# Seven products of quarters for the output projection, in one PSUM bank, and three shared staging buffers, in a two-layer transformer kernel

## The chip, the cores and the metric

One core of a Trainium2 chip runs the whole program. The metric is the device time of one execution in microseconds (us). All data are float32. In the text PE is TensorE (matmuls) and PEld its weight loads, DVE is VectorE, ACT is ScalarE, POOL is GpSimd, and SP is the engine whose queue issues nearly all DMAs.

## The reference

The kernel computes two layers for 4 batches of 1,024 rows of 512 features. The first is a graph attention with few neighbours, and the change does not touch it. The second is a transformer block with modulation:

```python
mod = silu(c) @ W_mod + b_mod
sh_msa, sc_msa, g_msa, sh_mlp, sc_mlp, g_mlp = split(mod, 6)
x = x + g_msa * attention(modulate(layernorm(x), sh_msa, sc_msa), W_qkv, W_out, b_out)
x = x + g_mlp * ff(modulate(layernorm(x), sh_mlp, sc_mlp), W1, b1, W2, b2)

# attention: 16 heads of 64
q, k, v = split(x @ W_qkv, 3)
attn = softmax(einsum('bqhd,bkhd->bhqk', q, k) * 64 ** -0.5)
out = einsum('bhqk,bkhd->bqhd', attn, v).reshape(B, T, 1024) @ W_out + b_out
```

What is changed is the last product, `@ W_out`, with the addition to the residual rows, and the staging of the softmax weights on their way to the product with `v`.

## The kernel before, in words

The attention stage goes through 256 slots: 4 batches, 8 pairs of heads `gp` in each, 8 blocks `t` of 128 query rows in each pair. So a batch has 64 slots, and two pairs of heads make one of four head groups `g`, with 16 slots.

In each slot the program issues, in this order: the transposition of the previous slot's first head on DVE (`turn`, L1119); evacuations of products that were put off (`later`); the scores of two heads into four PSUM banks (`scores`, L1084, tile `psc`); their maxima on DVE (`largest`, L1095); the exponentials with row sums on ACT (`weights`, L1101); reciprocals on DVE (L1106) and the scaling of the weights, the first head on ACT (L1108), the second on POOL (L1110); the transposition of the previous slot's second head; and then the work that a planner has put into this slot (`emit`). The next slot's scores need the banks back, so they wait for the exponentials.

`turn` writes into a staging tile `wd` of two blocks of rows. When the second block is in, four DMAs on SP's queue carry a head's tile to `wT` (L1123). Each of the two heads has two `wd` buffers of its own.

The planner's work in a slot is a list `fill` of entries (earliest slot, latest slot, units, place, function). They are:

- `attend`: the product of four slots earlier's weights with `v` (L1046, tile `pav`, 32 passes of 256 columns, in pairs at the same time), two units, evacuated by ACT into `oT` (L1055).
- `project`: 128 rows of the output projection for one head group (L1064, tile `pout`, four passes of 512 columns), one unit. DVE adds it to the residual rows `xr` (L1072); after the last group the rows are written to `x2d` (L1076) and their statistics taken.
- The chain of steps for q, k and v (`seven`, L520): products of a matrix multiplication by seven products of quarters instead of eight. Steps alternate on two banks `q1` and `q2`; their evacuations are put off to `later`, some on ACT, some on DVE (L534, L538). The sums of quarters of the weights are made on POOL (L491 to L494).
- Small ones: loads, gates, transpositions of normalized rows (`norm_T`, L430).

A matmul of float32 appears as two passes in the trace, so a `project` with two matmuls has four. `pav` and `pout` share the tag `mm` with two banks. `order_chain` chooses slots for the chain by dynamic programming on a cost that grows with the square of a slot's units, `order_others` moves the rest one by one. In a slot the entries are sorted by place: `attend` has 1, `project` 2, `norm_T` 3, gates and statistics 4, and a chain step 0.5, or 2.5 when the slot before also has one. The cost and the place are these:

```python
def cost_of(u, n):
    return u * u + 4 * max(n - 2, 0) ** 2
...
def place(k):
    if k in inside:
        return 2.5 if s - 1 in steps else 0.5
    return fill[k][3]
```

After the slots come the last projections among the first products of the MLP, and then the MLP of eight blocks of 512 rows. It uses the same seven products, with 256 columns.

Of the kernel before, what the change touches and what calls it, by code (L numbers as in the profile page):

```python
# [41 lines left out]
def cond_block_kernel(  # L42
# [880 lines left out]
    ps = pctx.enter_context(tc.tile_pool(name="ps2", bufs=1, space=PSUM))  # L923
    with ExitStack() as actx:
        ap_ = actx.enter_context(tc.tile_pool(name="ap", bufs=1, reuse_waits="tile"))
        MM = dict(tag="mm", bufs=2)
        q1, q2 = (ps.tile([P, F], F32, name=n, tag=n) for n in ("q1", "q2"))
        two_banks = {"ma": q2, "mb": q1, "mc": q1, "md": q2}
        NP = 2 * NGRP
# [6 lines left out]
        wout, gate = {}, {}  # L936
        vt, oT, xr, wn, wd, wT = {}, {}, {}, {}, {}, {}

        def bank(name):
            return ps.tile([P, F], F32, name=name, **MM)  # L940

        turns = []

        def bank_q(name):
# [4 lines left out]

        def load_out(b, g):  # L950

            t = op_.tile([P, 2, F], F32, name="wout", tag="wout", bufs=1)
            nc.sync.dma_start(t, w_out[g * GW : (g + 1) * GW, :].rearrange("(c p) f -> p c f", p=P))
            wout[b, g] = t

# [3 lines left out]
            for p in range(2):  # L959
                nc.gpsimd.tensor_tensor(t[:, p, :], t[:, p, :], gate[b][0], ALU.mult)  # L960

        def load_rows(b, n):

            t = op_.tile([P, F], F32, name="xr", tag="xr", bufs=NT)
            nc.sync.dma_start(t, x1d[b * NT + n])
            xr[b, n] = t

        def gate_rows(b, n):

            nc.gpsimd.tensor_tensor(xr[b, n], xr[b, n], gate[b][1], ALU.add)  # L970


        def gates_of(b):
# [62 lines left out]
                rhs=lambda which, n, c: of_weights(("v", b, g), wv[b, g], which, c),  # L1036
            )

        def attend(b, gp, k):

            po = ps.tile([P, QB], F32, name="pav", **MM)
            g, p = divmod(gp, 2)
            w = wT[b, gp, k]
            for m in range(KC):
                for j in range(2):
                    nc.tensor.matmul(  # L1046
                        po[j * D : (j + 1) * D, :],
                        lhsT=vt[b, g][:, m, p * P + j * D : p * P + (j + 1) * D],
                        rhs=w[:, j, :, m, :],
                        start=(m == 0),  # L1050
                        stop=(m == KC - 1),
                    )
            if k == 0:
                oT[b, gp] = op_.tile([P, S], F32, name="oT", tag="oT", bufs=3)
            nc.scalar.copy(  # L1055
                oT[b, gp][:, k * QB : (k + 1) * QB].rearrange("p (t u q) -> p u t q", t=QT, u=4),
                po.rearrange("p (u t q) -> p u t q", t=QT, u=4),
            )

        def project(b, g, n):  # L1060

            po = ps.tile([P, F], F32, name="pout", **MM)
            for p in range(2):
                nc.tensor.matmul(  # L1064
                    po,
                    lhsT=oT[b, 2 * g + p][:, n * P : (n + 1) * P],
                    rhs=wout[b, g][:, p, :],
                    start=(p == 0),
                    stop=(p == 1),
                )  # L1070
            t = xr[b, n]
            nc.vector.tensor_tensor(t, po, t, ALU.add)  # L1072
            if g == NGRP - 1:
                i = b * NT + n
                statistics(t, mv2[:, i, :], op_)
                nc.sync.dma_start(x2d[i], t)  # L1076


        def scores(b, gp, t):
# [32 lines left out]
        def turn(b, gp, t, j):  # L1112

            k, at = divmod(t, QT)
            if at == 0:
                wd[j] = ap_.tile([P, 4 * KC, QT, U], F32, name="wd", tag=f"wd{j}", bufs=2)
                if j == 0:
                    wT[b, gp, k] = ap_.tile([P, 2, 4, KC, QT * U], F32, name="wT", tag="wT", bufs=2)
            nc.vector.transpose(wd[j][:, :, at, :], wn.pop((b, gp, t, j)).rearrange("p (m k) -> p m k", k=U))  # L1119
            if at == QT - 1:  # L1120
                flat = wd[j].rearrange("p m t q -> p (m t q)")
                for u in range(4):
                    nc.sync.dma_start(  # L1123
                        wT[b, gp, k][:, j, u].rearrange("p m q -> p (m q)"), flat[U * u : U * (u + 1), :]
                    )
# [3 lines left out]
            return lambda: qp.tile([P, S], F32, name="ex", tag=tag, bufs=2)  # L1129

        def home_o():
            return op_.tile([P, S], F32, name="ex", tag="oT", bufs=3)

        def home_v():
            return vp.tile([P, NT, GW], F32, name="hs", tag="v", bufs=2)
# [10 lines left out]
        NS = B * NP * NT  # L1146
        LAG = 4

        chain = []

        def add(lo, hi, units, place, f, *args):
            fill.append((lo, hi, units, place, lambda: f(*args)))
# [15 lines left out]
        for b in range(B):  # L1168
# [22 lines left out]
            for gp in range(NP):  # L1191
# [13 lines left out]

                for k in range(NB):
                    lo = at + QT * k + LAG
                    add(lo, lo + (lo < NS - 8), 2, 1, attend, b, gp, k)
                if p == 1:
                    for n in range(NT):  # L1210
                        lo = at + max(QT * (n // 2) + LAG + 2 + (g == 0), 7)
                        hi = at + 19
                        if at == NS - NT:

                            lo = hi = NS + (-2, -1, -1, 0, 1, 1, 3, 3)[n]
                        add(lo, hi, 1, 2, project, b, g, n)
                if gp == 0:
                    lo = max(at - 1, 0)
                    add(lo, lo, 0, 0, gates_of, b)
                    for n in range(NT):  # L1220

                        lo = at + (1 + n if b == 0 else 14 + n // 2)
                        add(lo, lo, 0, 0, load_rows, b, n)
                        add(lo + 1, lo + 1, 0, 4, gate_rows, b, n)
                if p == 0:
                    add(at + 12, at + 12, 0, 0, load_out, b, g)
                    add(at + 13, at + 13, 0, 4, gate_out, b, g)
        add(3, 3, 0, 4, rstd, rs1, mv1, nm1, NT, NTA)

        add(NS - 20, NS - 20, 0, 4, rstd, rs2, mv2, nm2, 0, 3 * NT)  # L1230
# [20 lines left out]
        add(NS - 7, NS - 7, 0, 0, put_w1_rows)  # L1251
        add(NS - 8, NS - 8, 0, 4, mlp_rows)
        for i in range(4):
            at = NS - (10, 9, 6, 4)[i]
            home = (home_ex, home_q("qT"), home_q("kT"), home_o)[i]
            add(at, at, 0, 4, mlp_weights, nc.gpsimd, i, home)

# [14 lines left out]


        where = [f[0] for f in fill]
        inside = set(chain)

        def takes(k):

            return fill[k][2], int(k not in inside and fill[k][3] in (1, 2))

        def load_of(ks):
            used = {}
# [3 lines left out]
            return used  # L1286

        def cost_of(u, n):
            return u * u + 4 * max(n - 2, 0) ** 2

        def order_chain():

            used = load_of(k for k in range(len(fill)) if k not in inside)
            values = {where[k] for k, f in enumerate(fill) if f[3] == 1}
            first_steps = set(range(0, len(chain), 4))
            best = {(0, 0): (0, ())}
            for s in range(-8, NS):
                new = {}
                for (n, was), (cost, at) in best.items():
                    load, banks = used.get(s, (0, 0))  # L1300
                    for m in range(2):
                        extra = 0
                        if m > 0:
                            if n == len(chain) or not fill[chain[n]][0] <= s <= fill[chain[n]][1]:
                                break
                            load += fill[chain[n]][2]
                            if was and n not in first_steps and s not in values:
                                extra = 3
                        if n + m < len(chain) and fill[chain[n + m]][1] <= s:
                            continue  # L1310
                        c = cost + cost_of(load, banks) + extra
                        if (n + m, m) not in new or c < new[n + m, m][0]:
                            new[n + m, m] = c, (at, (s,) * m)
                best = new
            at = min((best[k] for k in best if k[0] == len(chain)), key=lambda v: v[0])[1]
            slots = []
            while at:
                at, part_ = at
                slots.append(part_)
            for k, s in zip(chain, [s for part_ in reversed(slots) for s in part_]):  # L1320
                where[k] = s
# [21 lines left out]
                    used[where[k]] = used.get(where[k], (0, 0))[0] + u, used.get(where[k], (0, 0))[1] + n  # L1343

        for _ in range(4):
            order_chain()
            order_others()
        for k, n, late in behind:
            where[k] = where[n] + late
# [12 lines left out]
        def emit(a, b):  # L1362


            for s in range(a, b):
                steps = {where[k] for k in chain}

                def place(k):
                    if k in inside:
                        return 2.5 if s - 1 in steps else 0.5  # L1370
                    return fill[k][3]

                for k in sorted(fill_of(s), key=lambda k: (place(k), k)):
                    fill[k][4]()
                if s in steps and s - 1 not in steps and sum(fill[k][2] for k in fill_of(s)) >= 3:
                    while later:
                        later.pop(0)()

        row_sum(0, 2)
        emit(-3, 0)  # L1380
        before = None
        for s in range(NS + 1):
# [4 lines left out]
            if s < NS:  # L1387
                b, r = divmod(s, NP * NT)
                gp, t = divmod(r, NT)
                sc = scores(b, gp, t)  # L1390
                mx = [largest(sc[j]) for j in range(2)]
                ws = [weights(sc[j], mx[j]) for j in range(2)]
                now = ((b, gp, t), ws)
                scaled(0, *ws[0])
# [212 lines left out]
```

## Time and profile before

| | before |
|---|---|
| median of three runs (lowest to highest) | 3060.71 us (3057.65 to 3062.03) |
| profiled execution | 3061.31 us, its span 3059.4 us |
| granted TensorE clock | 0.999 |
| matmuls of the output projection, L1064 | 512 passes, 245.5 us busy, mean 609 ns of one |
| its additions on DVE, L1072 | 128, 85.5 us busy, mean 678 ns |
| transpositions, L1119 | 512, 633.4 us busy |
| scores, L1084 | 415.3 to 2248.6 us of the span |

The durations are of one profiled execution, from the start of its span. Matmuls are pipelined: one lasts longer than the distance to the next, so what one costs is read from the distance of two starts. Idle time of an engine before an instruction is put down to what released it. A row of the timeline gives start, length, engine, line, operation, tiles and how many instructions are merged.

### The profile page before, as it was taken

Reading aid. Unit: us, or ns where it says so; the run is one execution under the profiler, and the core shown is the slowest. Engines: PE = TensorE matmul, PEld = TensorE weight load, DVE = VectorE, ACT = ScalarE, POOL = GpSimd, SP = SyncE. Lnnn points to the kernel's source line nnn. Section 1 sums busy time; section 2 is a strip of 40 time slices with the busy share of each in tenths; the row PEclk is TensorE's granted clock in tenths of the full one; section 3 lists DMA queues with packets and bytes.
Section 4 is the critical chain, followed back from the end, with each engine's and each line's share of the span. In section 5 each row is a group of like instructions: output and inputs, shape, how many; then the busy total and the mean of one; then the engine's idle time right before and its main releaser. Section 6 shows DMA issues by size and latency. Waiting matters only on the chain.

```text
span 3059.4 us, 40809 instructions
## 1 busy us (share of the span) xinstructions
PE 3025.6 (99%) x14967; PEld 1918.2 (63%) x14967; DVE 1957.9 (64%) x2743; ACT 1432.7 (47%) x2367; POOL 1213.8 (40%) x742
## 2 busy tenths in 40 slices
PE   9999999999999999999999999999999999999999
PEld 5666655455455455455455455455468888888888
DVE  3788867777878777878777878777764232222222
ACT  2444456556755555755555756556641221122211
POOL 1444455454555555555545555555531100111010
PEclk9999999999999999999999999999999999999999
DMA  6433448667777777877776877776772010101110
GB/s 194 133 122 112 133 107 199 152 159 179 187 181 189 178 167 170 193 182 183 180 174 159 200 185 174 182 175 152 192 192 93 14 49 28 49 14 42 35 42 14
DMA packets 282714, 418.00 MB, mean 137 GB/s; under 512 B 28912, under 2 KB 101036, under 8 KB 282516
## 3 DMA queue, kind: packets, MB, share of 16 engines
q1 hardware_dynamic: 282268, 415.06, 53.3%
q8 instruction: 120, 1.97, 0.3%
q14 instruction: 78, 0.64, 0.1%
q10 hardware_dynamic: 248, 0.34, 0.0%
HBM read 121.09 MB, written 25.76 MB: 48 GB/s over the span
## 4 chain that ended last, share of the span: by engine, by line
PE 84%; DVE 5%; ACT 3%; issue 2%; POOL 2%; SPq 2%; DMA 2%; POOLq 0%; ACTq 0%; DVEq 0%
PE q L520 18%; PE psc L1084 15%; PE pav L1046 14%; PE pout L1064 7%; PE mbd L520 5%; PE mbu L520 5%; PE mad L520 4%; PE mau L520 3%; PE mcd L520 2%; PE mdd L520 2%; PE mdu L520 2%; PE mcu L520 2%; PE pa L706 1%; ACT w L1101 1%; PE pf L666 1%
## 5 line engine op out<-in xcount | busy, mean ns | idle before, releaser
L1110 POOL TENSOR_SCALAR w<-w,sm 128x1024 f32<-128x1024 f32 x256 | 728.5, 2846 | 845.8 <-DVE sm L1106 844.5
L1101 ACT ACTIVATE w<-psc,mx 128x1024 f32<-128x1024 f32 x512 | 570.6, 1114 | 633.5 <-DVE mx L1095 633.5
L1119 DVE STREAM_TRANSPOSE wd<-w 128x1024 f32<-128x1024 f32 x512 | 633.4, 1237 | 131.5 <-ACT w L1108 117.8
L1095 DVE TENSOR_REDUCE mx<-psc 128x1 f32<-128x1024 f32 x512 | 599.3, 1211 | 123.0 <-PE psc L1084 121.2
L1084 PE MATMUL psc<-kT,qT 64*128 64x512 f32 x2048 | 529.9, 615 | 2.8 <-ACT kT L1010 1.4
L1046 PE MATMUL pav<-wT,v 128*64 128x256 f32 x4096 | 476.2, 382 | 2.0 <-DMA wT<-wd 1.2
L1046 PEld LDWEIGHTS pav<-wT,v 128*64 128x64 f32 x4096 | 294.7, 137 | 221.5 <-issue 66.9
L1084 PEld LDWEIGHTS psc<-kT,qT 64*128 64x128 f32 x2048 | 202.9, 186 | 254.4 <-issue 144.8
L1108 ACT ACTIVATE w<-w,sm 128x1024 f32<-128x1024 f32 x256 | 291.0, 1137 | 0.0
L499 POOL TENSOR_TENSOR tx<-hT 128x512 f32<-128x512 f32 x8 | 10.3, 1286 | 596.7 <-ACT hT L435 596.7
L1064 PE MATMUL pout<-wout,oT 128*128 128x512 f32 x512 | 245.5, 609 | 0.0
L520 PE MATMUL q<-hT,wqk 128*128 128x512 f32 (+1 forms) x396 | 182.6, 585 | 4.4 <-DVE q L534 4.4
L1064 PEld LDWEIGHTS pout<-wout,oT 128*128 128x128 f32 x512 | 90.2, 189 | 134.0 <-issue 119.1
L542 ACT COPY mbu<-mau 128x512 f32<-128x512 f32 x30 | 17.1, 570 | 276.5 <-PE mau L520 276.5
L706 PE MATMUL pa<-kp,sfT 128*128 128x320 f32 x512 | 143.5, 433 | 1.5 <-ACT sfT L681 1.5
L520 PEld LDWEIGHTS q<-hT,wqk 128*128 128x128 f32 x396 | 73.5, 190 | 100.6 <-issue 85.0
L1072 DVE TENSOR_TENSOR xr<-pout,xr 128x512 f32<-128x512 f32 x128 | 85.5, 678 | 79.1 <-PE pout L1064 79.0
L520 PE MATMUL q<-tx,ex 128*128 128x512 f32 (+1 forms) x264 | 125.0, 597 | 1.4 <-POOL tx L499 1.4
L706 PEld LDWEIGHTS pa<-kp,sfT 128*128 128x128 f32 x512 | 94.8, 190 | 38.2 <-ACT sfT L681 1.9
L666 PE MATMUL pf<-wx,xT 128*128 128x512 f32 x256 | 117.1, 601 | 0.0
L520 PE MATMUL mad<-w,hs 128*128 128x256 f32 x512 | 113.1, 379 | 0.0
L520 PEld LDWEIGHTS mad<-w,hs 128*128 128x128 f32 x512 | 97.3, 190 | 13.2
(284 smaller groups left out, 4222.7 us busy)
## 6 DMA issues: line engine op xcount, KB each, us to landing
wT<-wd SPq DMA_DIRECT2D x1024, 256.0 KB
wqk<-in_w_qkv SPq DMA_DIRECT2D x64, 256.0 KB
xT<-in_xt SPq DMA_DIRECT2D x32, 256.0 KB
xs<-in_x SPq DMA_DIRECT2D x32, 256.0 KB
x1d<-xs SPq DMA_DIRECT2D x32, 256.0 KB
xl<-x1d SPq DMA_DIRECT2D x32, 256.0 KB
wv<-in_w_qkv SPq DMA_DIRECT2D x32, 256.0 KB
xr<-x1d SPq DMA_DIRECT2D x32, 256.0 KB
```

Of the source, the lines that this page charges most:

```text
L520: nc.tensor.matmul(t[:, q * width : (q + 1) * width], lhsT=lhs(which, q, k), rhs=rhs(which, q, k), start=(fresh and q == 0 and k == 0), st ...
L666: nc.tensor.matmul(pfs[i], lhsT=xT[i][:, c, :], rhs=wx[:, c, :], start=False, stop=(c == FC - 1), skip_group_check=True,)
L706: nc.tensor.matmul(pas[i][:, n, :HF], lhsT=sfT2[i][:, c, :], rhs=kp[:, b, c, n * HF : (n + 1) * HF], start=False, stop=(c == FC - 1), skip ...
L1046: nc.tensor.matmul(po[j * D : (j + 1) * D, :], lhsT=vt[b, g][:, m, p * P + j * D : p * P + (j + 1) * D], rhs=w[:, j, :, m, :], start=(m == 0),
L1064: nc.tensor.matmul(po, lhsT=oT[b, 2 * g + p][:, n * P : (n + 1) * P], rhs=wout[b, g][:, p, :], start=(p == 0), stop=(p == 1),)
L1072: nc.vector.tensor_tensor(t, po, t, ALU.add)
L1084: nc.tensor.matmul(sc[j][:, n * F : (n + 1) * F], lhsT=qT[b, gp][q, t * P : (t + 1) * P], rhs=kT[b, gp][q, n * F : (n + 1) * F], start=Tru ...
L1095: nc.vector.tensor_reduce(mx, sc, axis=AX.X, op=ALU.max, negate=True)
L1101: nc.scalar.activation(w, sc, AF.Exp, bias=mx, accum_out=sm)
L1108: nc.scalar.mul(w, w, sm)
L1110: nc.gpsimd.tensor_scalar(w, w, sm, None, ALU.mult)
L1119: nc.vector.transpose(wd[j][:, :, at, :], wn.pop((b, gp, t, j)).rearrange("p (m k) -> p m k", k=U))
```

## The change

The projection of a head group (256 inputs, 512 outputs) is done for blocks `u` of 512 rows by seven products of quarters, two blocks in a group. `out_step` does one product: two matmuls (four passes) of 256 columns into the two halves of one bank `pu`, on top of what the bank holds or fresh, and then one DVE addition of the whole bank to a quarter of the residual rows, whose tile `xr` now holds 256 rows. Each step overwrites or extends the bank that the addition before it reads. POOL makes the sums of quarters: four for the weights of a group (`out_weights`), four for the rows of each block (`out_sums`). The last group of the last batch still goes by `project`.

`pav` and `pu` have one bank each in place of two shared ones. The steps form a second chain `outs` for `order_chain`, with windows of five or six slots, half a unit each and up to two in a slot. Of two steps in a slot the first is issued right behind the maxima (`early`), the second at the end of the slot (place 3.5). A slot with `attend` and nothing else on 128 rows and columns is charged 1.2 more for a step. In the seventh pair of heads of each batch an `attend` is cut into two halves in two slots.

The staging tiles `wd` of both heads share three buffers in place of four. `wout` has two buffers and is loaded four slots earlier, `oT` has six tiles of half the size, the loads of `xr` are at other slots, and one weight sum of the MLP comes a slot later.

The core of the diff:

```diff
-            t = op_.tile([P, 2, F], F32, name="wout", tag="wout", bufs=1)
+            t = op_.tile([P, 2, F], F32, name="wout", tag="wout", bufs=2)
...
-        def attend(b, gp, k):
-
-            po = ps.tile([P, QB], F32, name="pav", **MM)
+        pav = {}
+
+        def attend(b, gp, k, a=0, z=KC):
+
+            if a == 0:
+                pav[0] = ps.tile([P, F], F32, name="pav", tag="pav")[:, :QB]
+            po = pav[0]
...
+        PU = ((1, 1, (0, 0)), (0, 1, (0, 0)), (5, 0, (0, 1)), (6, 0, (1, 1)), (3, 0, (1, 0)), (4, 1, (1, 1)), (2, 0, (0, 1)))
+
+        def out_weights(b, g):
+
+            w = wout[b, g]
+            wsum[b, g] = op_.tile([P, 3 * HB], F32, name="wsum", tag="wsum", bufs=1)
+            o = [wsum[b, g][:, k * HB : (k + 1) * HB] for k in range(3)]
+            sums_b(nc.gpsimd, o, w[:, 0, :HB], w[:, 0, HB:], w[:, 1, :HB], w[:, 1, HB:])
+
+        def out_sums(b, g, u):
+
+            osum[b, g] = op_.tile([P, 3 * HB], F32, name="osum", tag="osum", bufs=1)
+            o = [osum[b, g][:, k * HB : (k + 1) * HB] for k in range(3)]
+            l, r = (oT[b, 2 * g + p, u] for p in range(2))
+            sums_a(nc.gpsimd, o, l[:, :QB], r[:, :QB], l[:, QB:], r[:, QB:])
+
+        def out_step(b, g, u, k):
+            which, fresh, (i, j) = PU[k]
+            if fresh:
+                pu[0] = ps.tile([P, F], F32, name="pu", tag="pu")
...
+            for q in range(2):
+                nc.tensor.matmul(
+                    pu[0][:, q * HB : (q + 1) * HB],
+                    lhsT=a[:, q * P : (q + 1) * P],
+                    rhs=r,
+                    start=(bool(fresh) and q == 0),
+                    stop=True,
+                    skip_group_check=True,
+                )
+            o = xr[b, 2 * u + i][:, :, j * HB : (j + 1) * HB]
+            nc.vector.tensor_tensor(o, pu[0].rearrange("p (r f) -> p r f", r=2), o, ALU.add)
...
-                wd[j] = ap_.tile([P, 4 * KC, QT, U], F32, name="wd", tag=f"wd{j}", bufs=2)
+                wd[j] = ap_.tile([P, 4 * KC, QT, U], F32, name="wd", tag="wd", bufs=3)
...
                     lo = at + QT * k + LAG
+                    if gp == NP - 2:
+
+                        for h in range(2):
+                            add(lo + h, lo + h, 1, 1, attend, b, gp, k, h * KC // 2, (h + 1) * KC // 2)
+                        continue
...
-                        lo = at + max(QT * (n // 2) + LAG + 2 + (g == 0), 7)
-                        hi = at + 19
...
+                    for u in range(2):
+                        for k in range(len(PU)):
+                            lo, hi = ((at + 8, at + 12), (at + 12, at + (15 if at == NS - 3 * NT else 17)))[u]
+                            if k == 0:
+                                behind.append((len(fill), len(fill) + 1, 0))
+                                add(-1, -1, 0, -1, out_sums, b, g, u)
+                            outs.append(len(fill))
+                            add(lo + k, hi + k, 0.5, 2, out_step, b, g, u, k)
...
-                        lo = at + (1 + n if b == 0 else 14 + n // 2)
-                        add(lo, lo, 0, 0, load_rows, b, n)
-                        add(lo + 1, lo + 1, 0, 4, gate_rows, b, n)
+                        lo = at + (1 + m if b == 0 else (12, 12, 17, 18)[m])
+                        add(lo, lo, 0, 0, load_rows, b, m)
...
-                    add(at + 12, at + 12, 0, 0, load_out, b, g)
-                    add(at + 13, at + 13, 0, 4, gate_out, b, g)
+                    add(at + 8, at + 8, 0, 0, load_out, b, g)
+                    add(at + 9, at + 9, 0, 4, gate_out, b, g)
...
-            at = NS - (10, 9, 6, 4)[i]
+            at = NS - (10, 9, 6, 3)[i]
...
-            return u * u + 4 * max(n - 2, 0) ** 2
+            return u * u + 4 * max(n - 1, 0) ** 2
...
-                    for m in range(2):
-                        extra = 0
+                    for m in range(2 if apart else 3):
+                        extra = 0.2 * (m == 2)
...
+                            if not apart and s in values and s not in others:
+
+                                extra += 1.2
...
+                second = [k for k in outs if where[k] == s][1:]
...
+                        if k in second:
+                            return 3.5
+                        return min(at, 2) + 0.1 if s in steps else 2
...
+        def early(s):
+
+            two = [k for k in outs if where[k] == s]
+            sums = [k for k in fill_of(s) if fill[k][3] == -1]
+            for k in two[: len(two) - 1] + sums:
+                fill[k][4]()
+                done_early.add(k)
...
                 mx = [largest(sc[j]) for j in range(2)]
+                early(s)
                 ws = [weights(sc[j], mx[j]) for j in range(2)]
```

## The prediction

> **What bounds the kernel now.** I read the engine totals first, then the engines over the attention stage, the PE's instructions in time order, the vector engine's in the same stretch, and last the waits. Totals, then the stage:
>
> ```profile
> PE 3025.6 (99%) x14967; PEld 1918.2 (63%) x14967; DVE 1957.9 (64%) x2743; ACT 1432.7 (47%) x2367; POOL 1213.8 (40%) x742
> ```
> ```profile
> 450.00:2250.00 1800.00, 1790.21 (x9199) 942.94 (x9196) 1397.73 (x1768) 1070.78 (x1667) 958.72 (x525) 1.00 0.74 179
> ```
> ```profile
> 1508.30 1.99 PE L1084 MATMUL psc<-kT,qT 64*128 64x512 f32 x8
> 1510.21 3.67 PE L1046 MATMUL pav<-wT,v 128*64 128x256 f32 x32
> 1513.82 2.18 PE L1084 MATMUL psc<-kT,qT 64*128 64x512 f32 x8
> 1515.93 1.98 PE L520 MATMUL q<-tx,ex 128*128 128x512 f32 x4
> 1517.75 1.88 PE L520 MATMUL q<-hT,wqk 128*128 128x512 f32 x4
> 1519.47 1.88 PE L1064 MATMUL pout<-wout,oT 128*128 128x512 f32 x4
> 1521.28 1.99 PE L1084 MATMUL psc<-kT,qT 64*128 64x512 f32 x8
> 1523.20 3.67 PE L1046 MATMUL pav<-wT,v 128*64 128x256 f32 x32
> 1526.80 2.60 PE L1084 MATMUL psc<-kT,qT 64*128 64x512 f32 x8
> ```
>
> The edit lies in the attention stage, where PE is busy 99.5% and DVE 78% of the time at a granted clock of 1.00. A slot runs from one psc row to the next. Its length is a sum of PE pieces: psc and pav alone 5.52 us (1508.30 to 1513.82), psc, eight q passes and one projection 7.46. Over all 255 slots, read the same way, psc with eight q passes takes 5.55, the same with a projection (four pout passes) 7.265, psc with pav and a projection 7.436. So a projection costs 1.717 us beside q passes (4 x 0.429), and 1.915 where it is alone with pav: 0.20 for one more change of tile shape. 64 slots make a batch of 452 to 462 us. Taking for each kind of slot its shortest example, 6 to 11 us of a batch are excess.
>
> That excess comes through DVE. Before the short slot at 1521.28 its queue is:
>
> ```profile
> 1521.39 0.69 DVE L1072 TENSOR_TENSOR xr<-pout,xr 128x512 f32<-128x512 f32 x1 [1.23 <-PE pout L1064]
> 1522.00 0.69 DVE L534 TENSOR_TENSOR q<-q,s 128x512 f32<-128x512 f32 x1
> 1522.60 1.23 DVE L1119 STREAM_TRANSPOSE wd<-w 128x1024 f32<-128x1024 f32 x1
> 1523.75 2.32 DVE L1095 TENSOR_REDUCE mx<-psc 128x1 f32<-128x1024 f32 x2
> ```
>
> A projection last in its slot holds back an add, a q evacuation and a transposition, so the maxima start 2.47 us after psc instead of 2.02. Exponentials come late, and as that slot is short, the next psc takes 2.60 instead of 1.99 to 2.18. A slot has about 5.5 us as its floor: psc to the first maximum 2.02, second maximum and second exponential over at 5.58 in most slots.
>
> **The change, part by part.**
>
> *Projection to seven products.* 15 of 16 head groups change; the last keeps eight projections. Removed: 120 projections x 1.717 = 205.9 us, and 20 shape changes beside pav x 0.20 = 4.0. Added: 15 x 2 x 7 = 210 steps of four passes over 256 columns. The stage has hardly any such pass, but the MLP has:
>
> ```profile
> 2402.21 1.89 PE L520 MATMUL mbu<-tx,ex 128*128 128x256 f32 x8
> 2403.94 1.89 PE L520 MATMUL mau<-hT,w 128*128 128x256 f32 x8
> ```
>
> Eight passes from 2402.21 to 2403.94 are 0.216 each, half of 0.429 and 1 to 2 ns. So 840 x 0.216 = 181.4. Bounds: 0.216, and 0.24 if each step's first pass is 0.10 longer, as the first psc or pout pass behind another shape is. I take 0.216 where a step stands beside q passes.
>
> The Trainium skill, page "TensorE: Matmul & The Clock Gate", section "Back-to-back issue gap", speaks against small passes: in a stream of weight loads and matmuls the spacing is set by both, and it gives 81 ns instead of 56 for 128 columns. By an estimate from it, 25 ns on each of 840 passes would be 21 us, nearly the whole saving; the MLP rows, with a load before every pass, show 1 to 2 ns, and the measurement decides.
>
> *Where the steps land.* I laid the 14 steps of a group onto the slots by the diff's cost rule, with the present slots as loads. In a batch some 17 slots of q without pav take two (one right behind psc, one at the end), 14 slots take one beside q or a transposition, three slots with half a pav take two. Slots with a full pav alone take none. A q slot with two steps is 5.548 + 8 x 0.216 = 7.28, as long as one with a projection now; the gain comes from having fewer such slots, pav with a projection falling from 7.436 to 5.52.
>
> *Half pavs.* In the seventh head pair of a batch four pavs become eight halves in slots 52 to 59. That adds some nine changes of shape in a batch, including those of a step on each side of a half: 9 x 4 x 0.20 = 7.2 us.
>
> *One bank pu.* A step waits for DVE's add of the step before; behind it wait all matmuls, so the next psc. In a two-step q slot the first ends about 2.9 us into the slot, its add follows the second maximum (4.3 to 5.0), the second starts at 6.3: 1.3 us of cover. Without the cover, in the three slots with half a pav, it is due near 4.9: 0.3 x 3 x 4 = 3.6 us. The separate bank pav costs nothing: the next pav is at least a psc (1.9 us) away, and its ACT copy takes 0.36.
>
> *DVE.* 210 adds for 120, 90 x 0.678 = 61 us. The stage has 1800 - 1398 = 402 us of idle DVE, so the sum is covered; the order is not. Two-step slots ahead of a lone pav give the picture of 1521.39 above. In 3 such places of a batch the q step before has a DVE evacuation (slots 19, 25 and 13); two of them pay already, and the run of slots 12 to 16, which loses 2 us now, gets work to fill it. Net I take 0 (bounds -1 to +10 us a batch).
>
> *POOL.* Twelve sums of 256 columns a group, 15 x 12 x 0.73 = 131 us. POOL is busy 959 of 1800 and waits mostly for reciprocals:
>
> ```profile
> L491 POOL TENSOR_TENSOR ex<-wqk 128x256 f32<-128x256 f32 x33 | 24.1, 729 | 1.5 <-PE q L520 1.5
> POOL w L1110 <- DVE sm L1106: 844.5, 237, 7.2
> ```
>
> Activation sums are issued behind the maxima and need 2.9 us; the scaling they precede becomes ready some 5.8 us into the slot, and only the third product needs them. Zero; if POOL were late by all four sums, a transposition would be 2.9 late, in up to 30 slots.
>
> *Three staging buffers.* The first transposition of a pair's second head now needs the buffer whose DMAs left a slot earlier. From the semaphore updates of each DMA, the first head's four transfers have landed a median 7.8 us after its transposition; that later one starts a median 10.0 after it. The smallest margin over 126 pairs is 0.44 us, so as the slots stand it costs 0. If landings came 0.7 us later, 9 pairs would wait for less than 0.4 us each; 1.5 us later, 32 pairs, 14 us in all. DVE already waits now and then:
>
> ```profile
> DVE wd L1119 <- DMA wT<-wd: 4.8, 6, 0.9
> ```
>
> Behind that wait stand a reciprocal, the next transposition and the next maxima, so only a short slot passes it on.
>
> *Moved loads.* wout loads come four slots earlier, into two buffers; the residual rows still are 32 transfers, for the last two tiles a slot or two behind the stores that free them. The wT transfers stand behind them in SP's queue: 0, at most 3 us in each of three batches. The last MLP weight sums are one slot later: +1 us (0 to 3), at the end PE needs them about a slot after.
>
> **Sum.** -205.9 - 4.0 + 181.4 + 7.2 + 3.6 + 1 = -16.7 us. The profiled execution took 3061.3 (span 3059.4 and 1.9 around it), 0.6 above the median 3060.7; 3060.7 - 16.7 = 3044.0.
>
> **Rivals.**
>
> *DVE's tail at the end of a slot eats the gain (slower).* Price 0.6 us, from the psc of 2.60. It decides from (16.7 + 6) / 0.6, about 38 more such places, ten a batch. For it: 77 slots of the stage are under 6.2 us, and the second step's add can't start before PE ends the slot. Against: half of the q steps are evacuated by ACT alone, and long slots absorb the delay. At 60 places: 3044 + 36 = 3080. Chance 0.14.
>
> *The staging buffer becomes the wait.* With 14 us of DVE waits passed on: 3058, no change. For it: a margin of 0.44 and DMA engines 74% busy. Chance 0.08.
>
> *A step costs more than half a projection.* If each of 210 steps pays the 0.10 of a first pass: 21 us, 3065, no change. The rule of the Trainium skill above would end at the same time. Against: q after pout starts without it. Chance 0.06.
>
> *The planner's steps don't land as I laid them*, with half of them beside pavs and two changes of shape each: 105 x 0.4 = 42, so 3086. Chance 0.03.
>
> *The present excess is filled up by half units*, 2 to 3 us a batch: 3033. Chance 0.07.
>
> **The numbers.** The forecast, 3044 (own range 3034 to 3053), has 0.62. A measurement can tell 0.2%, 6 us, from no change. Faster: 0.62 + 0.07 and a third of the staging case, 0.72; slower: 0.14 + 0.03, 0.17; the rest, 0.11, the same. The range runs from 3032 to 3070: it leaves out half of the first rival and the planner's.
>
> **What would show it.** Right: psc, two pu steps and eight q passes near 7.28 us; pu passes at 0.216; pav alone near 5.52; batches near 457 us; 210 adds of about 0.68; no DMA wait of note before the transpositions. Wrong: psc rows of 2.6 us and more all over, maxima later than 2.02 us after psc in most slots, PE waits at pu for the add, idle time of transpositions put down to wT<-wd, or pu passes at 0.24.

## The result

The changed kernel takes 3044.25 us in the median of four runs (3043.45 to 3045.16), against 3060.72 before (3057.65 to 3062.03): 16.5 us less, a ratio of 0.9945 with a 95% interval of 0.9933 to 0.9957. The forecast was 3044.0. The profiled execution took 3043.88, its span 3041.9; before it was 3061.31 and 3059.4.

The engines' totals of the changed kernel, then its attention stage in the same stretch as before:

```profile
PE 3004.2 (99%) x15327; PEld 1977.4 (65%) x15327; DVE 1996.9 (66%) x2833; ACT 1430.9 (47%) x2367; POOL 1338.3 (44%) x922
```
```profile
450.00:2250.00 1800.00, 1786.25 (x9636) 1012.14 (x9633) 1447.57 (x1874) 1078.94 (x1684) 1087.90 (x708) 1.00 0.75 180
```

PE is still busy 99% of that stretch, DVE has gone from 78% to 80%, POOL from 53% to 60%. The distance from the first psc to the last fell from 1833.7 to 1816.5 us, 17.2 us; what lies before and behind it kept 1225.8 and 1225.4. So the whole change of time is in the stage.

PE in the changed kernel, in time order, a slot with two steps, a lone pav and the psc of the slot behind it (start, length, engine, line, operation, tiles, number merged):

```profile
1044.18 2.19 PE L1139 MATMUL psc<-kT,qT 64*128 64x512 f32 x8
1046.30 1.13 PE L1122 MATMUL pu<-wout,oT 128*128 128x256 f32 x4
1047.27 1.88 PE L520 MATMUL q<-tx,ex 128*128 128x512 f32 x4
1048.98 1.88 PE L520 MATMUL q<-hT,wqk 128*128 128x512 f32 x4
1050.70 1.03 PE L1122 MATMUL pu<-wout,oT 128*128 128x256 f32 x4
1051.65 1.99 PE L1139 MATMUL psc<-kT,qT 64*128 64x512 f32 x8
1053.57 3.67 PE L1047 MATMUL pav<-wT,v 128*64 128x256 f32 x32
1057.18 2.60 PE L1139 MATMUL psc<-kT,qT 64*128 64x512 f32 x8
```

The last pu step has 0.95 us to the next psc (1050.70 to 1051.65). From psc to psc it is 7.47 us, 0.20 of it a late psc (2.19 for 1.99); the shortest slot of this kind is 7.275, forecast was 7.28. The lone pav behind it takes 5.53, and the psc after it 2.60 instead of 1.99: the same loss behind a short slot as at 1526.80 before, from the same queue on DVE:

```profile
1051.76 0.69 DVE L1131 TENSOR_TENSOR xr<-pu,xr 128x512 f32<-128x512 f32 x1 [1.02 <-PE pu L1122]
1052.37 0.69 DVE L534 TENSOR_TENSOR q<-q,s 128x512 f32<-128x512 f32 x1
1052.97 1.24 DVE L1174 STREAM_TRANSPOSE wd<-w 128x1024 f32<-128x1024 f32 x1
1054.13 2.32 DVE L1150 TENSOR_REDUCE mx<-psc 128x1 f32<-128x1024 f32 x2
```

The groups of the page that answer to those of before, and the waits for staging and bank in the stage, DVE's and PE's:

```profile
L1131 DVE TENSOR_TENSOR xr<-pu,xr 128x512 f32<-128x512 f32 x210 | 143.4, 683 | 79.5 <-PE pu L1122 79.3
```
```profile
DVE wd L1174 <- DMA wT<-wd: 2.9, 4, 0.9
```
```profile
PE pu L1122 <- DVE sm L1161: 4.1, 9, 1.0
...
PE pu L1122 <- DVE xr L1131: 1.6, 4, 1.0
```

There are 210 additions of 0.683 us, and 2.9 us of waiting for a staging buffer where it was 4.8. PE waits 5.7 us ahead of pu steps (a wait is put down to the DVE instruction that ended nearest to it): 3.1 us of it in slot 9 of three batches, which the last experiments take up, the rest in slots 51, 54 and 56 of the batches. The granted clock is 1.00 throughout the stage, as before.

### The profile page after: what moved, and what is told of

Read it like the earlier page. It is cut to its first block, busy times and chain, and to the rows that moved or that the text cites. A ratio compares the mean times of both kernels' runs of the same rounds, so it can differ in the third digit from the quotient of the medians.

```text
span 3041.9 us, 41802 instructions
## 1 busy us (share of the span) xinstructions
PE 3004.2 (99%) x15327; PEld 1977.4 (65%) x15327; DVE 1996.9 (66%) x2833; ACT 1430.9 (47%) x2367; POOL 1338.3 (44%) x922
## 3 DMA queue, kind: packets, MB, share of 16 engines
q8 instruction: 123, 2.02, 0.3%
## 4 chain that ended last, share of the span: by engine, by line
PE 81%; DVE 7%; ACT 4%; issue 3%; POOL 2%; DMA 2%; SPq 1%; POOLq 0%; DVEq 0%; ACTq 0%
PE q L520 18%; PE psc L1139 14%; PE pav L1047 13%; PE mbd L520 5%; PE pu L1122 5%; PE mbu L520 5%; PE mad L520 4%; PE mau L520 3%; ACT w L1156 2%; PE mcd L520 2%; PE mdd L520 2%; DVE mx L1150 2%; PE mdu L520 2%; PE mcu L520 2%; POOL t L729 1%
## 5 line engine op out<-in xcount | busy, mean ns | idle before, releaser
L1131 DVE TENSOR_TENSOR xr<-pu,xr 128x512 f32<-128x512 f32 x210 | 143.4, 683 | 79.5 <-PE pu L1122 79.3
L1122 PE MATMUL pu<-wout,oT 128*128 128x256 f32 x360 | 98.4, 396 | 4.2 <-DVE sm L1161 2.2
L1122 PEld LDWEIGHTS pu<-wout,oT 128*128 128x128 f32 x360 | 62.6, 189 | 59.2 <-issue 31.6
```

The costliest lines, as they stand in the source:

```text
L1122: nc.tensor.matmul(pu[0][:, q * HB : (q + 1) * HB], lhsT=a[:, q * P : (q + 1) * P], rhs=r, start=(bool(fresh) and q == 0), stop=True, skip ...
L1131: nc.vector.tensor_tensor(o, pu[0].rearrange("p (r f) -> p r f", r=2), o, ALU.add)
```

## The experiments

Each kernel was timed against the kernel before on the same chip; the median of that was 3060.6 to 3061.2 in all sessions. Differences from the changed kernel are taken from its 3044.25 us above. The theory is that of the prediction: the time is the sum of PE's pieces, and DVE, POOL and the staging have cover as long as the order leaves it. The rivals were the order of the slots, DVE's tail, and the staging buffer.

**e1_before_three: the staging alone.** The kernel before with

```diff
-wd[j] = ap_.tile([P, 4 * KC, QT, U], F32, name="wd", tag=f"wd{j}", bufs=2)
+wd[j] = ap_.tile([P, 4 * KC, QT, U], F32, name="wd", tag="wd", bufs=3)
```

> The kernel before, with the three shared staging buffers as the only edit. Theory (the time is the sum of PE's work, staging keeps a margin of at least 0.44 us): 3060.7 us, within 2 us, and no more than 5 us of DVE waiting for wT<-wd in all. Rival (the staging buffer costs and the products gain more than the result shows): 5 to 15 us more, 3066 to 3076.

Measured: 3061.47 us, ratio 1.0000 (0.9992 to 1.0009). DVE waits 6.6 us for wT<-wd in the stage, 1.8 more than before and 1.6 over the bound that was set, and the time doesn't move. The fourth buffer was worth nothing.

**e7_two_buffers: one buffer less.** The changed kernel with `bufs=2`.

> The changed kernel with two shared staging buffers in place of three. From the landings in the trace of the changed kernel the first transposition of a pair would start before its buffer is free in all 126 pairs, by 2.9 us in the median, 374 us in all. Theory (DVE in order passes nearly all of it to the maxima): 3300 us (3150 to 3450). Rival (DVE's idle time and long slots swallow it): under 3100.

Measured: 3264.32 us (3261.67 to 3266.96, two runs), 220 us more than the changed kernel. DVE's waits in this kernel from 450 to 2400 us:

```profile
DVE wd L1174 <- DMA wT<-wd: 450.6, 181, 5.3
```

So the wait is real and expensive as soon as the margin is negative; three buffers are just enough. In the changed kernel the smallest margin, from landing to the transposition that needs the buffer, was 0.12 us (0.44 with the slots of the kernel before), none negative. Not all of the 220 us is the wait itself. In this kernel's stage the granted clock falls to 0.50 in 22 stretches of 3.4 or 6.8 us, 116 us in all, where in the changed kernel it never does; at half the clock that is an estimated 58 us at most. A fourth buffer in the changed kernel was not tried.

**e2_eighth: eight products again.** The first product of each block is done twice into the fresh bank:

```diff
-for q in range(2):
-    nc.tensor.matmul(pu[0][:, q * HB : (q + 1) * HB], ...)
+for n in range(2 if k == 0 else 1):
+    for q in range(2):
+        nc.tensor.matmul(pu[0][:, q * HB : (q + 1) * HB], ...)
```

> The changed kernel, with the first product of each block of 512 rows done twice into its fresh bank: eight products of work for seven, 30 more products, everything else as it is. Theory (PE's passes set the time): 30 x 4 x 0.216 = 25.9 us more than the changed kernel, 3070 us (3066 to 3074). Rival (the gain is one of order, of banks and slots, and PE has room): 3044 to 3050 us.

Measured: 3064.30 us (3062.76 to 3067.34), 20.0 more than the changed kernel and 1.0011 (1.0002 to 1.0020) of the kernel before. The rival falls: without the eighth product saved, nothing of the gain is left. The 20.0 are below 25.9 and below the stated 22 to 30, because part of the passes fell into time that PE lost anyway. The excess over the shortest slot of each kind fell by 7.2 us, from 35.9 to 28.7; slot 9 of a batch for instance went from 1.49 to 0.63. The stage grew by 19.6 us. Without that fall it would have grown by 26.8, close to the 25.9 of the added passes.

**e3_adjacent: the steps not held apart.** Both steps of a slot come at its end:

```diff
-for k in two[: len(two) - 1] + sums:
+for k in sums:
...
-if k in second:
+if len([n for n in outs if where[n] == s]) == 2:
     return 3.5
```

> The changed kernel, with both steps of a slot that has two at its end, one right behind the other (no early step). Theory: the second waits for the addition of the first with nothing of PE between: about 0.04 to the addition, 0.68 for it, 0.1 to the next pass, less what the pipeline hides, so about 1.0 us lost in each of 84 slots, and a second addition in the tail on DVE: 3128 us (3105 to 3160). Rival (holding the steps apart is not what makes the bank cheap; PE hides the wait or the slots are longer than PE's work anyway): under 3060 us.

Measured: 3146.09 us, ratio 1.0278 (1.0264 to 1.0292), 102 us more than the changed kernel: 1.2 in each slot that has two steps (the trace has 83 of them, where 84 had been counted). PE in this kernel, then its waits in the stage:

```profile
1027.33 1.03 PE L1122 MATMUL pu<-wout,oT 128*128 128x256 f32 x4
1029.14 1.13 PE L1122 MATMUL pu<-wsum,osum 128*128 128x256 f32 x4 [0.79 <-DVE xr L1131]
```
```profile
PE pu L1122 <- DVE xr L1131: 80.3, 79, 2.7
```

The second step begins 1.81 us after the first, where its four passes alone would need 0.86 (4 x 0.216). 80.3 of the 102 us are such waits. Up to 10 us more, by an estimate, come from six stretches of 3.4 us in which the granted clock is 0.50; what the rest is stays open. The single bank is cheap only because other matmuls lie between two steps.

**e6_whole_pav: no halves.** The branch that cuts pav in the seventh pair is taken out; the planner lays the steps anew.

```diff
-if gp == NP - 2:
+if False:
```

> The changed kernel without the cutting of pav in the seventh pair of heads; the planner lays the steps anew. Theory (the halves cost shape changes, 7.2 us, and waits for additions, 3.6 us): 3038 us (3033 to 3044), the halves are a cost. Rival (the halves give cover between two steps and even out slots that PE would otherwise wait in): slower than the changed kernel, 3047 to 3060 us.

Measured: 3056.81 us (3054.66 to 3059.72), ratio 0.9987 (0.9978 to 0.9996): 12.6 us *more* than the changed kernel, against my expectation. PE of this kernel, at the end of a batch:

```profile
1261.66 1.99 PE L1139 MATMUL psc<-kT,qT 64*128 64x512 f32 x8
1263.58 1.13 PE L1122 MATMUL pu<-wsum,osum 128*128 128x256 f32 x4
1266.78 1.17 PE L1122 MATMUL pu<-wout,osum 128*128 128x256 f32 x4 [2.07 <-DVE sm L1161]
1267.88 3.56 PE L1139 MATMUL psc<-kT,qT 64*128 64x512 f32 x8
```

The slots between whole pavs hold no chain step. With two pu steps and nothing between, PE waits 2.07 us for the first addition, which stands behind the maxima. The psc behind it takes 3.56 us instead of 1.99 for another reason: from 1267.7 to 1271.1 the granted clock is 0.50. That happens three times in this kernel's stage, each time 0.6 to 0.9 us after the end of a wait of 2.1 to 2.2 us, and costs about 1.6 us; in the changed kernel no wait of PE in the stage reaches 1.5 us. In all, PE waits 20.3 us ahead of pu instead of 5.7. Changes of tile shape fall from 628 to 590, 7.6 us less at 0.20 each; 14.6 more of waits and some 4.7 of slow clock outweigh them, 11.7 us net, against 10.8 between the two profiled executions. I had counted the shape changes of the halves and left out that they are the cover of the steps there. As the planner lays the steps, three quarters of the gain hang on them; it laid all steps anew here (90 slots with two steps instead of 83), so the halves aren't the only difference.

**e4_more_dve: more work on DVE.** Behind each addition:

```diff
+extra = ap_.tile([P, 1], F32, name="mxx", tag="mxx", bufs=2)
+nc.vector.tensor_reduce(extra, pu[0], axis=AX.X, op=ALU.max, negate=True)
```

> The changed kernel, with one more DVE reduction of the pu bank to one column behind each of the 210 additions, its result unused: about 0.6 us each by half of the maximum's 1.21, 126 us more of DVE. Theory (DVE's sum has room, its tail at the end of a slot is paid only ahead of a short slot): 15 to 40 us more, 3070 us (3058 to 3085). Rival (DVE has room enough, the tail is covered): 3044 to 3050. Second rival (DVE is the bound of the stage already): over 3130.

Measured: 3075.71 us (3073.01 to 3077.78), 31.5 more than the changed kernel, for 117 us more of DVE by the page (2114.0 against 1996.9; one took 0.68, not 0.6). So DVE is not the bound by its sum, and not free either: beyond the work of the changed kernel a microsecond of this work costs 0.27. But the reduction also reads the bank, so the next step has to wait for it: PE waits 25.0 us ahead of pu in the stage where the changed kernel has 5.7, most of it in slots 51 to 57. So some 19 of the 31.5 us are waits for the bank. What DVE work that leaves the bank alone would cost is not shown.

**e11_fewer_adds: less work on DVE.**

```diff
-nc.vector.tensor_tensor(o, pu[0].rearrange(...), o, ALU.add)
+if k not in (2, 3, 5):
+    nc.vector.tensor_tensor(o, pu[0].rearrange(...), o, ALU.add)
```

> The changed kernel without the additions of three of the seven steps (the third, fourth and sixth), which leaves their parts out of the result: 90 additions, 61 us of DVE, as many as the change added, and the waits of three steps for them. Theory by the kernel with more DVE work (31 us for 126 of DVE): 15 us less, 3029 us (3024 to 3036). Rival (the prediction: DVE's additions net to 0, only 3.6 us of waits in slots with half a pav): 3040 us (3038 to 3044).

Measured: 3043.95 us (3041.86 to 3047.35), ratio 0.9947 (0.9934 to 0.9959): no change from 0.9945. By the page DVE is busy 45 us less (1951.5 against 1996.9), not the 61 of their added lengths. 90 additions, as many as the change put on DVE, cost nothing, as the prediction had it, and a price taken from more work (e4) doesn't hold for less. Waits that the missing additions might have saved gave nothing either.

**e5_more_pool and e10_no_sums: POOL, both ways.** In e5 the first operation of each sum is done four times more, here in `out_sums` and likewise in `out_weights`:

```diff
+for _ in range(4):
+    nc.gpsimd.tensor_tensor(o[0], l[:, QB:], r[:, QB:], ALU.add)
 sums_a(nc.gpsimd, o, l[:, :QB], r[:, :QB], l[:, QB:], r[:, QB:])
```

and in e10 `sums_a` and `sums_b` are left out of `out_sums` and `out_weights`, and the products read quarters in place of the sums.

> The changed kernel, with the first of the four POOL operations done four times more in each of 45 sums: 45 x 4 x 0.73 = 131 us more of POOL, as much again as the change added. Theory (POOL has cover): 3044 us, within 3. Rival (the activation sums hold up the scaling and with it the second transposition): 10 us or more, over 3054.

> The changed kernel without POOL's twelve sums of quarters a group; the products take quarters in place of the sums, so the projection is left wrong. 131 us less of POOL, the same passes and additions. Theory (the sums as they are have cover; only twice as many were late): 3042 us (3038 to 3045). Rival (each sum is paid for as in the kernel with more POOL work, 11 us for 131): 3033 us (3030 to 3036).

Measured: 3055.30 us (3052.30 to 3065.84) with 131 us more, ratio 0.9986 (0.9978 to 0.9995); 3043.37 (3041.95 to 3047.43) with the sums left out, ratio 0.9946 (0.9934 to 0.9959). So the sums as they are have cover, and twice as many don't: my expectation for e5 was wrong. There DVE's waits in the stage have a line that is 2.6 us in the changed kernel (it is the wait of the transpositions for POOL's scaling):

```profile
DVE wd L1178 <- POOL w L1169: 53.3, 37, 2.8
```

The scaling comes late behind the sums, and with it the second transposition.

**e9_spread_rows, e12_no_stats, e13_late_stats: the row statistics.** Two places of the changed kernel lose what the kernel before didn't: slots 9 and 11 of the second to fourth batch, 1.49 and 1.05 us over the shortest of their kind. DVE there, from the start of slot 9 at 928.45:

```profile
928.71 0.68 DVE L111 BATCH_NORM_STATS2 st<-xr 128x6 f32<-128x512 f32 x1
...
931.80 0.18 DVE L112 BATCH_NORM_AGGREGATE mv<-st 128x2 f32<-128x6 f32 x1
932.01 1.25 DVE L1174 STREAM_TRANSPOSE wd<-w 128x1024 f32<-128x1024 f32 x1
933.18 2.32 DVE L1150 TENSOR_REDUCE mx<-psc 128x1 f32<-128x1024 f32 x2
```

The statistics of four row tiles come together, since both last steps of a block are in slot 7, and the maxima start 4.7 us after psc instead of 2.02. Before, the statistics came one to a slot. e9 gives them to four slots:

```diff
-behind.append((len(fill), outs[-1], 1))
+late_ = 1 + r + 2 * (k - 5) if u == 0 else 1 + r * (6 - k)
+behind.append((len(fill), outs[-1], late_))
```

> The changed kernel, with the four row statistics that a batch's last group takes in one slot (slot 8) given to slots 8 to 11 one by one. Theory (slots 9 and 11 are 1.49 and 1.05 us over their shortest example in three batches, because DVE does 3.3 us of statistics before the transposition and the maxima of slot 9): 5 to 7.6 us less than the changed kernel, 3038 us (3036 to 3041). Rival (these slots wait for POOL's activation sums or for the pu bank, and the statistics have cover): no change, 3043 to 3046.

Measured: 3044.37 us (3042.60 to 3047.55), ratio 0.9950 (0.9936 to 0.9964): nothing gained. In the trace slot 9 fell from 1.49 to 0.20 in three batches, 3.9 us in all. Slots 10 to 12 took up about half of it (in the second batch they lose 0.23, 1.18 and 1.25, in the changed kernel nothing, 1.05 and 1.10), slots 16 to 18 another 1.2 us. So it isn't the bunching alone. e12 puts a memset in place of twelve of the statistics.

> The changed kernel without the statistics of four rows' tiles in each of the first three batches (a memset in their place, so the normalization of these rows is left wrong): 12 statistics, some 10 us of DVE, in slots 8 and 9. Theory (DVE is full in slots 8 to 11: 27.8 us of work in 25.6 us of PE's pieces, which is why spreading the statistics gave nothing): the excess of slots 9 and 11 goes, 2.5 us in each of three batches, 3037 us (3035 to 3039). Rival (something else holds these slots): 3043 to 3045.

Measured: 3037.31 us (3036.44 to 3045.49), ratio 0.9924 (0.9911 to 0.9938), 6.9 less than the changed kernel for some 10 us of DVE (8.5 by the page, with the memsets in their place). The two intervals overlap a little (that of the changed kernel begins at 0.9933), so the size is less sure than the direction. Slots 9 and 11 fell to 0.29 and less in the profiled execution. That one is the slowest of the five, 3045.49: it lost 6 us elsewhere, in two slots of the first batch in which the granted clock was 0.50 for 6.8 us. The 27.8 us of work in the expectation adds up lengths that overlap; slots 8 to 11 of the changed kernel are busy 25.4 us on DVE for 25.6 of PE's pieces, which still is full. Here, between two-step slots and lone pavs, DVE has next to no room, and its work was paid for in both places where it was put. e13 therefore takes it out of the stage:

```diff
-statistics(t, mv2[:, i, :], op_)
+if b in (0, B - 1):
+    statistics(t, mv2[:, i, :], op_)
...
+if p == 1 and 2 <= nxt < 6:
+    for n in range(nxt * VB, (nxt + 1) * VB):
+        statistics(xl[1, n], mv2[:, n, :], mp2)
 if p == 2 and nxt < NB2:
+    if 2 <= nxt < 6:
+        rstd(rs2, mv2, nm2, nxt * VB, (nxt + 1) * VB)
     norm_rows(1, nxt)
```

> The changed kernel, with the row statistics of the second and third batch taken in the MLP, from the rows that it loads for its blocks 2 to 5, ahead of their normalization; there DVE is busy 2 to 3 tenths. Nothing is left out. Theory (DVE is full where the last group of a batch ends): 2.5 us less in two batches and part of the excess of slots 16 to 18, 3037 us (3034 to 3041), the fastest so far. Rival (the statistics and a square root on ACT with its table loads hold up the MLP): 3044 to 3056.

Measured: 3041.33 us (3039.88 to 3044.13), ratio 0.9936 (0.9922 to 0.9949). The stage is 3.7 us shorter in the profiled execution (1812.8 against 1816.5), and what lies behind it 0.3 longer. It beats the kernel before; over the changed kernel the 2.9 us of the medians are within the two intervals, so that step is likely, not certain. It fell short of 3037 because slot 11 kept 0.61 of its 1.05, and because the batch whose statistics stay loses as before.

## Why the prediction was right, point by point

**PE bounds the stage, and the time is the sum of its pieces.** Right. Taking the shortest example of each kind of slot, as in the prediction, the stage's pieces fell by 17.5 us (1796.7 to 1779.2, from the first psc row to the 256th), and the excess over them stayed, 35.6 before and 35.9 after. The shortest examples hold the waits that every slot of their kind has. With each pass and each change of shape priced alone, the stage's work fell by 21.5 us, where these terms of the sum make 21.3 (205.9 + 4.0 - 181.4 - 7.2), and all waits together rose by 4.2, where the sum has 3.6. e2 gives the price from the other side.

**A pass of 256 columns costs 0.216.** Right: inside a step the median distance of two starts is 216 ns, with a weight load before every pass. The 25 ns more that the prediction had estimated from the Trainium skill didn't show.

**A change of shape costs 0.20.** It holds in the changed kernel. The Trainium skill, page "TensorEngine Tiling (Array Packing)", section "Key Properties", says that changing the tiling mode drains the engine; the trace agrees, and it gives the number: 0.09 us before the first pass behind a change and 0.10 in it. The stage has 612 changes before and 628 after, the 36 added and 20 removed of the sum.

**Where the steps land.** Nearly right: 70 slots of q with two steps (17.5 a batch, 17 forecast), 13 with half a pav and two steps (3 a batch forecast), 44 single ones (14 a batch forecast, 11 came), none beside a lone pav.

**Half pavs and the bank pu.** The 36 changes of 7.2 us are there. For the 3.6 us at the bank the trace has 5.7 us of waits ahead of pu, but 3.1 of them stand in slot 9, which the prediction hadn't named, and 2.7 in slots 51, 54 and 56. What the halves meant was missing: as e6 shows, without the halves the time is 12.6 us more.

**DVE's additions and POOL's sums at 0.** Right, by e11 and e10. But DVE's net 0 came about otherwise than written, and that it came out is luck: the statistics in slots 8 and 9 weren't seen, they cost about 2.5 us in each of three batches, and the excess of other slots (13, 14 and 50, up to 2 us a batch together) went away. Of these the prediction had named the run of slots 12 to 16, but not slot 50.

**Staging at 0.** Right, by e1, and e7 shows how near the edge it is. In the trace before, landings 0.7 us later would have made 6 pairs wait, not 9, by less than 0.3 us each.

**The last weight sums at +1.** Not seen: what lies behind the last psc took 810.4 us in both.

**The rivals.** DVE's tail exists (2.60 at 1057.18), but in about as many places as before: 17 psc groups of 2.4 us and more against 16. It would have needed more work than the change brings (e4). The 77 slots under 6.2 us in its favour are the slots of kinds whose shortest example is under 6.2; 67 are under it themselves. The first-pass price is paid by a step only where a q step would have paid it in its place, so a two-step slot has its 7.275.

## What to carry to other kernels

Where one engine is busy all the time, write the slot as a sum of its pieces, price each from the distance of starts of the same shape, and check it against the shortest slots of each kind; this sum came within 0.3 us of 3044, the last few microseconds of it by luck, since two unseen terms on DVE nearly cancelled. Other engines' work is free only as far as there is room: POOL's sums cost nothing when they were left out and 0.08 of their time when as much again was added; the additions on DVE cost nothing when 45 us of them were left out, and 117 us of further work cost 0.27 of its time, part of it through the bank. So room must be tested upwards. A bank shared by a chain of steps needs other work of that engine between two steps, and edits that look like a cost of their own, as the halves here, may be that cover.

## What the runs showed that was not expected

DVE was busy only 80% of the stage and yet had stretches without any room: some 10 us of statistics cost 6.9 there, and spreading them out saved nothing (e12, e9), while 90 additions over the whole stage, 45 us of busy time, cost nothing (e11). The SBUF to SBUF transfers of the first head's 1 MB landed 7.8 and 7.9 us (median) after its transposition in the two kernels, so a buffer less turned a margin of 0.12 us into 220 us of time (e7). And a wait of PE can cost twice: in e6 each of three waits of 2.1 to 2.2 us was followed by 3.4 us at a granted clock of 0.50, and in e3 and e7 such stretches came among many waits, while in the stage of the kernel before and of the changed kernel, where no wait of PE is longer than 1.4 us, there is none.
